# Token mixes with one product each, and expert weights that may come from DRAM, in a macaron transformer on one Trainium2 core

## The chip, the cores and the metric

The kernel runs on one core of one Trainium2 chip. The metric is the device time of one launch in microseconds (us). A core has five engines with instruction streams of their own: TensorE (PE, matrix products), VectorE (DVE), ScalarE (ACT), GpSimd (POOL) and SyncE (SP, which here only issues transfers). They wait for each other by semaphores. Data lie in DRAM, in the on-chip memory SBUF (128 partitions) and in PSUM (the 8 accumulator banks that PE writes). DMA transfers move data between DRAM and SBUF.

## The reference

The input has 8 sequences of 256 tokens with 128 features, so 2048 tokens. Six residual steps follow each other, each on a layer norm of the running `x`:

```
x = x + 0.5 * moe(layernorm(x))          # 8 experts, hidden 352, top 2 per token
x = x + attention(layernorm(x))          # 16 heads of 8, causal
x = x + 0.5 * moe(layernorm(x))          # same weights as the first
x = x + 0.5 * mix(layernorm(x))
x = x + shift(layernorm(x))              # 9 gated, rolled copies, then a layer norm
x = x + 0.5 * mix(layernorm(x))          # same weights as the first mix
```

The step that the change is mainly about is `mix`. Each token is blended with the token before it (zeros ahead of the first token of a sequence), feature by feature, with two different blends:

```
x_prev = concatenate([zeros, x[:, :-1]], axis=1)
xr = mu_r * x + (1 - mu_r) * x_prev
xk = mu_k * x + (1 - mu_k) * x_prev
r   = sigmoid(xr @ W_r.T)
k   = xk @ W_k.T
out = r * (square(relu(k)) @ W_v.T)
```

## The kernel before

**Tiling.** The tokens form four groups of 512 (`NG`), each held as `x[g]` with 4 tiles of 128 tokens (`GT`). Nearly every step works on one group. A product of 128 features by 512 tokens is one instruction of the program for PE, which the hardware runs as two, since the data are 32-bit floats.

**Order.** The program first describes all steps as operations with an engine, an expected duration, the operations they need and the buffers they take. `Work.issue` then lists them: it goes through the ready operations, takes the one that can start first by its own reckoning, and prefers higher ranks. The order on every engine is fixed by this. An `either` operation goes to ScalarE or VectorE, whichever would be done first (`LEAN` adds to the reckoned time of an engine). Numbers in `BIAS` shift the rank of whole groups: entries 0 to 3 rank the four groups in the last part of the program, 4 and 5 the two parts of the second expert layer's routing, 6 the later part of the first one's. Where PE would stand still by the reckoning, `keep_warm` inserts filler products (`pw`) into an unused bank. Line numbers in the profile are those of one helper (L71) for nearly all instructions, so tiles are known by their names.

**Expert layers** (`moe_route`, `moe_plan`, `moe_experts`, `moe_back`). Tokens are routed, a plan (counts, places, lookup products `pi`) sorts them by expert into 36 tiles of 128 rows, and each tile consists of two halves of 64 rows, called units, each with one expert. Rows are fetched by indirect DMA on POOL's queue (`xs`), transposed and scaled (`nT`), multiplied by the gate and up weights (`pg`, `pu`), gated (`sg`, `hid`), transposed (`ph`, `hT`), multiplied by the down weights (`po<-dw,hT` and `po<-wd,hT`) and stored to DRAM (`ys`, on SP's queue). Later `moe_back` fetches each token's two rows (`back`, POOL's queue) and adds them to `x`. The plan has two parts: the first two groups' tokens fill 12 tiles, which can start before the other groups are routed.

All weights of all experts stay in SBUF: `gu` (128 x 8 x 704) and `dw` (128 x 8 x 384). The first unit of a tile reads its expert's weights there, by a register on PE. For the second unit, `copied` (line 1073) copies the expert's weights into `wg` or `wd` (three buffers each) by an `either` operation, with the expert number in a register of the copying engine. There are 72 + 72 such copies, 89 on ScalarE and 55 on VectorE.

`dw`'s rows lie in three blocks of 128 that start at `HC` = (0, 128, 224), so the third block starts with rows 224 to 255, which are already in the second. Therefore `dw[0:32, :, 2, :]` is set to zero on VectorE and the third block is loaded for partitions 32 to 127 alone.

**Mix** (line 1569). For one group: moments, a power on POOL, normalising on ScalarE into `y`, transposing on PE into `pt`, and a copy into `yTs` (one zero column ahead of each sequence), so that the token before is the same data one column to the left. The blend lies in the weights: `mix_weights` (line 1802) makes `wkp`, `wkk`, `wrp` and `wr` once, with six VectorE steps, and each of the two results is a sum of two products:

```
for k, weight in enumerate((wkp, wkk)):
    nc.tensor.matmul(
        pk, lhsT=weight, rhs=yT.out[:, :, k : k + S], start=(k == 0), stop=(k == 1)
    )
```

`pr` is built in the same way, in 4 tiles with two products each. Then `rk` (relu) and `ka` (square) on ScalarE, `pv` on PE, `r` (tanh) on ScalarE, `rv` on VectorE, and an addition into `x[g]` on POOL. There are eight mixes: two for each group.

**Shift** (line 1653). Nine gate products `pgt`, each with a tanh on ScalarE and a product with the shifted values on VectorE (`p` or `q`). `FOLD[g]` says how they are summed: a number m means that m of them are first added pairwise on POOL, and each such sum then goes through `total` on PE, four products with the identity that add into the bank `po`. Group 0's (4, 4, 1) has three `total`s and six POOL additions.

Of the kernel before, what the change touches and what calls it, by code (L numbers as in the profile page):

```python
# [13 lines left out]
AF = mybir.ActivationFunctionType  # L14
# [20 lines left out]

BIAS = (32.0, 24.0, 8.0, 17.0, 27.0, 19.0, -1.0)
HC = (0, 128, 224)
ROUND = float(3 * 2**22)  # L40
NH = 16
# [9 lines left out]


ASIDE = ((3,), ())
FOLD = ((4, 4, 1), (2, 2, 2, 2, 1), (4, 4, 1), (2, 2, 2, 2, 1))


TB, DB = 1, 1
LEAN = {"act": 0.0, "dve": 0.15}


class InOrder:
# [47 lines left out]
class Op:  # L109
    def __init__(self, engine, us, do, needs, takes, uses, lag, spare):  # L110
        self.engine, self.us, self.do, self.lag, self.spare = engine, us, do, lag, spare
        self.takes, self.uses = takes, uses
        self.needs = [n for n in needs if n is not None]
        self.out, self.end, self.rank, self.back = None, None, None, 0.0
        self.strips = False
        self.choice = None


class Work:
# [14 lines left out]
    def op(self, engine, us, do=None, needs=(), takes=(), uses=(), lag=0.0, spare=0):  # L134
# [8 lines left out]
        self.ops.append(op)  # L143
        return op

    def either(self, act, dve, do, *needs, **kw):

        op = self.op("act", min(act, dve), None, needs, **kw)
        op.choice = {"act": act, "dve": dve}
        op.do = lambda: do(op.engine)  # L150
        return op
# [6 lines left out]
    def start(self, op):  # L158
        if op.choice is None:
            return self.start_on(op)  # L160
        best = None
        for engine, us in op.choice.items():
            op.engine = engine
            t = self.start_on(op)
            if t is None:
                return None
            us += LEAN.get(engine, 0.0)
            if best is None or t + us < best[0]:
                best = (t + us, t, engine)
        op.engine, op.us = best[2], op.choice[best[2]]  # L170
        return best[1]


# [98 lines left out]
def tile_macaron(ctx: ExitStack, tc: tile.TileContext, a: dict, out: bass.AP):  # L272
# [9 lines left out]
    def ctile(name, shape, dtype=F32):  # L282
        return const.tile(shape, dtype, tag=name, name=name)
# [10 lines left out]
        nc.sync.dma_start(out=x[g], in_=xv[g])  # L294
    gu = ctile("gu", [P, E, 2 * HID])
    dw = ctile("dw", [P, E, len(HC), P])

    nc.vector.memset(dw[0:32, :, 2, :], 0.0)
    half = E // 2
    nc.sync.dma_start(out=gu[:, 0:half, :], in_=a["guT"][:, 0:half, :])  # L300
    nc.sync.dma_start(out=dw[:, :, 0:2, :], in_=a["dwT"][:, :, 0:2, :])
    nc.sync.dma_start(out=dw[32:P, :, 2, :], in_=a["dwT"][32:P, :, 2, :])
    nc.sync.dma_start(out=gu[:, half:E, :], in_=a["guT"][:, half:E, :])


# [8 lines left out]
    rest = ctile("rest", [P, width])  # L314
    wd, wup, wuv, wo, wr, wkk, wv, vw, gw = (rest[:, c] for c in parts.values())
    wup = wup.rearrange("p (h r) -> p h r", r=32)
    wkp, wrp = ctile("wkp", [P, P]), ctile("wrp", [P, P])
    gamma = ctile("gamma", [P, P])
    beta = ctile("beta", [P, P])

# [16 lines left out]
    with nc.allow_low_precision("zeros and ones"):  # L337
# [34 lines left out]
    nc.vector.tensor_scalar(ha, ha, -0.5, 2.0, ALU.max, ALU.min)  # L372
    nc.vector.tensor_scalar(ha, ha, 0.5, None, ALU.mult)

    spare = ctile("spare", [P, 1])
    nc.scalar.activation(spare, one8[:, 0:1], AF.Silu)

# [10 lines left out]
        buffers={  # L388
            "b": 8, "xs": 3, "nT": 3, "y": 2, "nTr": 1, "sg": 2, "hid": 2, "hT": 2, "ys": 4,
            "at": 2, "ata": 1, "back": 2, "cT": 2, "av": 2, "o": 2, "oT": 2, "qk": 2, "ep": 4, "mtmp": 2,  # L390
            "t": 11, "q": 10, "p": 4, "mix": 2, "yTs": 2, "yTg": 2, "wg": 3, "wd": 3, "vT": 2,
        },
        free={"pool": 3.3, "dve": 3.3, "act": 2.5, "sp": 3.5, "pe": 2.6},
    )
# [14 lines left out]
    def copies(engine, dst, src):  # L409
        if engine == "act":  # L410
            nc.scalar.copy(dst, src)
        else:
            nc.vector.tensor_copy(dst, src)
# [6 lines left out]
    def wtile(tag, name, shape, dtype=F32):  # L420
        return wk.tile(list(shape), dtype, tag=tag, name=name, bufs=len_of[tag])
# [641 lines left out]
    def moe_tile(r, plan, k, nT, nb, j, pus, turned, downs, numbers):  # L1063
# [7 lines left out]


        def copied(engine, tag, src, width):
            e = {"act": nc.scalar, "dve": nc.vector}[engine].number(
                r["expert"][0:1, 2 * k + 1 : 2 * k + 2]
            )
            dst = wtile(tag, tag, (P, width))
            src = src[:, bass.ds(e, 1)].rearrange("p o h -> p (o h)")
            copies(engine, dst, src)
            return dst  # L1080

        gb, db = Buf("wg"), Buf("wd")
        gates = w.either(
            1.1, 0.9, lambda e: copied(e, "wg", gu, 2 * HID), plan["experts"], weights,
            *pus[-3:-2], takes=[gb],
        )
        backs = w.either(
            0.84, 0.74, lambda e: copied(e, "wd", dw.rearrange("p e c d -> p e (c d)"), len(HC) * P),
            plan["experts"], weights, *pus[-3:-2], takes=[db],
        )  # L1090

# [477 lines left out]
    def mix(g, n):  # L1569

        token = Buf("mix")
        y, filled = norm(
            g, n, "t", lambda: stile("t", "y"), switched, split=0, takes=[token]
        )
        b1, yb = Buf("b"), Buf("yTs")
        pt = w.pe(0.44, lambda: transposed(filled[0].out), *filled, takes=[b1], uses=[y], spare=1)

        def keep(engine):
            yT = stile("yTs", "yTs", (P, 2, S + 1))
            if engine == "act":  # L1580
                nc.scalar.activation(yT[:, :, 0:1], one8[:, 0:2].unsqueeze(2), AF.Copy, scale=0.0)
            else:
                nc.vector.memset(yT[:, :, 0:1], 0.0)
            copies(engine, yT[:, :, 1 : S + 1], pt.out.rearrange("p (b t) d -> p b (t d)", b=2))
            return yT

        yT = w.either(0.8, 0.76, keep, pt, takes=[yb], uses=[b1])
        b2, b3, b4 = Buf("b"), Buf("b"), Buf("b")


        def keys():
            pk = bank([P, 2, S], "pk")
            for k, weight in enumerate((wkp, wkk)):
                nc.tensor.matmul(
                    pk, lhsT=weight, rhs=yT.out[:, :, k : k + S], start=(k == 0), stop=(k == 1)
                )
            return pk.rearrange("p b s -> p (b s)")

        def receptances():
            out = bank([P, GT, P], "pr")  # L1600
            for t in range(GT):
                for k, weight in enumerate((wrp, wr)):
                    at = (t % 2) * P + k
                    nc.tensor.matmul(
                        out[:, t, :], lhsT=yT.out[:, t // 2, at : at + P], rhs=weight,
                        start=(k == 0), stop=(k == 1),
                    )
            return out

        def outcomes():  # L1610
            out = bank([P, GT, P], "pv")
            for t in range(GT):
                nc.tensor.matmul(
                    out[:, t, :], lhsT=ka.out[:, bass.ts(t, P)], rhs=wv, start=True, stop=True
                )
            return out

        pk = w.pe(1.76, keys, yT, weights_mixed, takes=[b2], uses=[yb], spare=2)
        pr = w.pe(1.8, receptances, yT, weights_mixed, takes=[b3], uses=[yb], spare=1)
        rkb, rrb, kab, rvb = (Buf("t") for _ in range(4))  # L1620

        def bent(name, src, function, shape):
            dst = stile("t", name, shape)
            nc.scalar.activation(dst, src, function, scale=0.5)
            return dst

        rk = w.act(
            0.6, lambda: bent("rk", pk.out, AF.Relu, (P, GT * P)), pk, takes=[rkb], uses=[b2]
        )
        r = w.act(  # L1630
            0.6, lambda: bent("r", pr.out, AF.Tanh, (P, GT, P)), pr, takes=[rrb], uses=[b3]
        )

        def square():
            ka = stile("t", "ka", (P, GT * P))
            nc.scalar.square(ka, rk.out)
            return ka

        ka = w.act(0.55, square, rk, takes=[kab], uses=[rkb])
        pv = w.pe(0.9, outcomes, ka, takes=[b4], uses=[kab])  # L1640

        def receptance():
            rv = stile("t", "rv")
            nc.vector.scalar_tensor_tensor(rv, r.out, 1.0, pv.out, ALU.add, ALU.mult)
            return rv

        rv = w.dve(0.7, receptance, r, pv, takes=[rvb], uses=[rrb, b4])
        changes(g, w.pool(
            1.3, lambda: nc.gpsimd.tensor_tensor(x[g], x[g], rv.out, ALU.add), rv,
            *tokens[g].given, *tokens[g].read, uses=[rvb, token],  # L1650
        ))
# [147 lines left out]

    rest_loaded = w.sp(1.5, load_rest, *(r0["stored"][g] for g in first), lag=8.0)  # L1800

    def mix_weights():

        for to, own, mu in ((wkp, wkk, mu_k), (wrp, wr, mu_r)):
            nc.vector.tensor_scalar(to, own, mu, None, ALU.mult)
            nc.vector.tensor_tensor(to, own, to, ALU.subtract)
            nc.vector.tensor_tensor(own, own, to, ALU.subtract)

    moe_plan(r0, False)
    w.back = -BIAS[6]  # L1810
    for g in range(len(first), NG):
        moe_route(g, r0)
    moe_plan(r0, True)
    w.back = 0.0
    weights_mixed = w.dve(2.0, mix_weights, rest_loaded, fewer, r0["plan"][1]["slots"])
    for groups in (first, list(range(len(first), NG))):
        moe_weights(groups, r0, r0["plan"][1]["taken"])
    stored = moe_experts(r0, [[1, 1, 2, *turns(r0["few"] - 4)], turns(TILES - r0["few"])])
# [97 lines left out]
```

## Time and profile before

| | us |
|---|---|
| median of 3 runs | 506.69 (506.56 to 506.85) |
| profiled execution | 506.38 |
| its span, first to last instruction | 504.6 |
| PE busy | 485.7 |
| VectorE busy | 355.0 |
| ScalarE busy | 285.0 |
| POOL busy | 225.3 |
| first expert product `pg` starts | 32.7 |
| first `pk` of a mix starts | 385.4 |
| last expert tile's products end | about 410 |
| last `total` ends | 485.2 |

The profile describes one execution. Durations of single instructions are read from it, and matmuls are pipelined, so the distance from start to start counts rather than the duration. Us from the span's start tell where a stretch lies. "Granted clock" is the share of full clock that TensorE was given.

### The profile page before, as it was taken

How to read it: one execution, taken by the hardware profiler on the slowest of the kernel's cores; microseconds unless marked ns; L12 is line 12 of the kernel's file. 1: busy time of each engine (PE TensorE's matmuls, PEld its weight loads, DVE VectorE, ACT ScalarE, POOL GpSimd, SP SyncE). 2: the span in 40 equal slices, each digit the busy share in tenths (PEclk: the TensorE clock that was granted, in tenths of full speed). 3: DMA queues.
4: the chain of work that ended last, by engine and by line, in shares of the span. 5: the costliest groups of instructions: out<-in, count | busy, mean ns of one | idle time of the engine just before them, and what ended most of it. 6: DMA issues, size and time to landing. Idle time of an engine off the chain costs nothing.

```text
span 504.6 us, 13830 instructions
## 1 busy us (share of the span) xinstructions
PE 485.7 (96%) x5199; PEld 317.9 (63%) x5199; DVE 355.0 (70%) x1207; ACT 285.0 (56%) x589; POOL 225.3 (45%) x240
## 2 busy tenths in 40 slices
PE   7979999999999999999999999799999999999995
PEld 4525667665676667776777766566665664665773
DVE  7847777678757886678786267946777657998561
ACT  3337666575365464455556567346767756557452
POOL 7154588472016500000037000278776858866362
PEclk9869999999999999999999799789999999999998
DMA  8841222221001100000202001032232211000001
GB/s 269 303 137 38 65 58 62 72 59 45 12 22 49 40 1 3 4 22 2 66 17 62 11 2 43 13 84 62 49 75 58 58 33 38 0 2 0 21 22 42
DMA packets 25984, 25.53 MB, mean 51 GB/s; under 512 B 3872, under 2 KB 23328, under 8 KB 25504
## 3 DMA queue, kind: packets, MB, share of 16 engines
q1 hardware_dynamic: 20368, 15.21, 9.8%
q0 software_dynamic: 4352, 8.92, 6.8%
q8 instruction: 42, 0.69, 0.5%
q10 hardware_dynamic: 1200, 0.53, 0.4%
q14 instruction: 22, 0.18, 0.1%
HBM read 16.78 MB, written 8.91 MB: 51 GB/s over the span
## 4 chain that ended last, share of the span: by engine, by line
PE 77%; DVE 13%; issue 3%; POOL 2%; DMA 2%; ACT 1%; POOLq 0%; DVEq 0%
PE sc L71 17%; PE po L71 16%; PE pg L71 9%; PE pu L71 9%; PE ph L71 5%; PE pt L71 5%; PE pgt L71 3%; PE pr L71 3%; PE pk L71 2%; DVE st L71 2%; PE pv L71 2%; DVE stats L71 2%; PE pj L71 2%; POOL back L71 2%; DMA xs<-rows,take 1%
## 5 line engine op out<-in xcount | busy, mean ns | idle before, releaser
L71 POOL DMA_INDIRECT xs<-rows,take x72 | 70.2, 975 | 48.7 <-issue 15.1
L71 POOL DMA_INDIRECT back<-ys,slot x64 | 61.9, 967 | 55.1 <-issue 45.2
L71 ACT ACTIVATE ep<-sc 128x512 f32<-128x512 f32 x96 | 52.3, 594 | 53.3 <-PE sc L71 53.3
L71 POOL TENSOR_TENSOR stats<-stats,minus_half 128x4 f32<-128x4 f32 x28 | 29.1, 1038 | 105.0 <-DVE stats L71 104.2
L71 PE MATMUL pg<-gu,nT 128*64 x144 | 58.3, 487 | 0.2
L71 PE MATMUL pg<-wg,nT 128*64 128x352 f32 x144 | 58.3, 487 | 0.0
L71 PEld LDWEIGHTS sc<-kT,qT 32*128 32x128 f32 x768 | 46.1, 186 | 19.1 <-issue 16.6
L71 PE MATMUL sc<-qT,kT 32*128 32x128 f32 x768 | 57.9, 288 | 0.1
L71 PE MATMUL pu<-gu,nT 128*64 x144 | 56.1, 472 | 0.3 <-PE pi L71 0.3
L71 PE MATMUL pu<-wg,nT 128*64 128x352 f32 x144 | 56.1, 472 | 0.0
L71 PE MATMUL sc<-kT,qT 32*128 32x128 f32 x768 | 55.5, 284 | 0.0
L71 PE MATMUL po<-dw,hT 128*64 x432 | 55.4, 279 | 0.0
L71 PE MATMUL po<-wd,hT 128*64 128x128 f32 x432 | 55.4, 279 | 0.0
L71 ACT ACTIVATE sg<-pg 128x352 f32<-128x352 f32 x72 | 33.3, 462 | 37.9 <-PE pg L71 25.9
L71 PEld LDWEIGHTS po<-dw,hT 128*64 128x64 f32 x432 | 48.6, 139 | 8.5 <-issue 6.4
L71 DVE TENSOR_REDUCE mtmp<-sc 128x4 f32<-128x512 f32 x64 | 41.4, 683 | 16.9 <-PE sc L71 16.8
L71 PEld LDWEIGHTS sc<-qT,kT 32*128 32x128 f32 x768 | 48.4, 190 | 3.4 <-issue 2.7
L71 PEld LDWEIGHTS po<-wd,hT 128*64 128x64 f32 x432 | 48.7, 139 | 0.0
L71 DVE TENSOR_TENSOR hid<-sg,pu 128x352 f32<-128x352 f32 x72 | 36.6, 515 | 15.9 <-PE pu L71 8.4
L71 ACT COPY wg<-gu 128x704 f32 x45 | 35.0, 779 | 13.8 <-PE pu L71 7.2
L71 PE MATMUL pgt<-yTg,rest 128*128 128x512 f32 x72 | 34.1, 600 | 1.1 <-DVE p L71 0.9
L71 PE MATMUL ph<-ident,hid 128*128 128x128 f32 x216 | 32.3, 285 | 0.3 <-DVE hid L71 0.3
(225 smaller groups left out, 1067.4 us busy)
## 6 DMA issues: line engine op xcount, KB each, us to landing
ys<-ys SPq DMA_DIRECT2D x72, 64.0 KB, 1.6
gu<-in_guT SPq DMA_DIRECT2D x2, 1408.0 KB, 8.4
rest<-in_rest SPq DMA_DIRECT2D x1, 1280.0 KB
xs<-rows,take POOLq DMA_INDIRECT x72, 2.5
x<-in_x SPq DMA_DIRECT2D x4, 256.0 KB
dw<-in_dwT SPq DMA_DIRECT2D x1, 1024.0 KB
rows<-rows SPq DMA_DIRECT2D x2, 512.0 KB
back<-ys,slot POOLq DMA_INDIRECT x64, 2.6
```

Source lines behind the costliest of these rows:

```text
L71: ins = do(*args, **kw)
```

## The change

Four things are changed.

1. **Mix.** `yTs`, `wkp`, `wrp` and `mix_weights` go. Two blended token tiles, `xk` and `xr`, are made in SBUF for each mix, in two steps each: `earlier_token` (on ScalarE or VectorE) writes the token before, times one minus mu, with zeros ahead of the first; `own_token` (VectorE) adds the token itself times mu, read from `pt`. `pk` is then one product, and `pr` one for each of the four tiles. One small step on VectorE (`less`) makes 1 - mu at the start.
2. **Weights of second units.** `copied` gets a third possibility, SP: a transfer from DRAM straight into `wg` or `wd`, with the expert number in a register of SP. The ordering reckons 1.9 and 1.2 us on SP for them, 2.6 us more until they land, and `LEAN` subtracts 2.5.
3. **`dw`.** Its DRAM image has the zeros for the overlapping rows, so the `memset` goes, and `dw` is loaded whole by one transfer.
4. **Numbers.** `BIAS` and `FOLD` are new, and `yTs` has four buffers in place of two.

In the order that results, 20 of the 144 weight copies are on SP (4 `wg`, 16 `wd`), 75 on ScalarE and 49 on VectorE. `earlier_token` is 11 times on ScalarE and 5 times on VectorE. There are 21 `total`s in place of 16, and 15 POOL additions in place of 20. Fillers `pw` are 100 in place of 94; behind the last `total` there are 29 in place of 18.

```diff
-BIAS = (32.0, 24.0, 8.0, 17.0, 27.0, 19.0, -1.0)
+BIAS = (25.0, 33.0, 10.0, 5.0, 15.0, 53.0, -5.0)
...
-FOLD = ((4, 4, 1), (2, 2, 2, 2, 1), (4, 4, 1), (2, 2, 2, 2, 1))
+FOLD = ((2, 2, 2, 1, 1, 1), (2, 2, 2, 1, 1, 1), (4, 4, 1), (2, 2, 2, 1, 1, 1))
...
-LEAN = {"act": 0.0, "dve": 0.15}
+GATES, BACKS, LANDING = 1.9, 1.2, 2.6
+LEAN = {"sp": -2.5, "act": 0.0, "dve": 0.15}
...
-    nc.vector.memset(dw[0:32, :, 2, :], 0.0)
...
-    nc.sync.dma_start(out=dw[:, :, 0:2, :], in_=a["dwT"][:, :, 0:2, :])
-    nc.sync.dma_start(out=dw[32:P, :, 2, :], in_=a["dwT"][32:P, :, 2, :])
+    nc.sync.dma_start(out=dw, in_=a["dwT"])
...
+            if engine == "sp":
+                src = {"wg": a["guT"], "wd": a["dwT"].rearrange("p e c d -> p e (c d)")}[tag]
             src = src[:, bass.ds(e, 1)].rearrange("p o h -> p (o h)")
-            copies(engine, dst, src)
+            if engine == "sp":
+                nc.sync.dma_start(out=dst, in_=src)
+            else:
+                copies(engine, dst, src)
...
-        yT = w.either(0.8, 0.76, keep, pt, takes=[yb], uses=[b1])
+        def by_own(name, own, other):
+            cb = Buf("yTs")
+            def earlier_token(engine):
+                c = stile("yTs", name, (P, 2, S))
+                src = pt.out.rearrange("p (b t) d -> p b (t d)", b=2)[:, :, 0 : S - 1]
+                if engine == "act":
+                    nc.scalar.activation(
+                        c[:, :, 0:1], one8[:, 0:2].unsqueeze(2), AF.Copy, scale=0.0
+                    )
+                    nc.scalar.activation(c[:, :, 1:S], src, AF.Copy, scale=other)
+                else:
+                    nc.vector.memset(c[:, :, 0:1], 0.0)
+                    nc.vector.tensor_scalar(c[:, :, 1:S], src, other, None, ALU.mult)
+                return c
+            c = w.either(0.8, 0.76, earlier_token, pt, takes=[cb], uses=[b1])
+            def own_token():
+                nc.vector.scalar_tensor_tensor(
+                    c.out, pt.out.rearrange("p (b t) d -> p b (t d)", b=2), own, c.out,
+                    ALU.mult, ALU.add,
+                )
+                return c.out.rearrange("p b s -> p (b s)")
+            return w.dve(0.7, own_token, c, uses=[b1, cb]), cb
+        xk, xkb = by_own("xk", mu_k, less_k)
+        xr, xrb = by_own("xr", mu_r, less_r)
...
+            nc.tensor.matmul(pk, lhsT=wkk, rhs=xk.out, start=True, stop=True)
...
+                nc.tensor.matmul(
+                    out[:, t, :], lhsT=xr.out[:, bass.ts(t, P)], rhs=wr, start=True, stop=True
+                )
```

## The prediction

> **What bounds the kernel now.** I read the page's head first, then its busy line, then one table by stretches, then the chain that ended last near the end.
>
> ```profile
> span 504.6 us, 13830 instructions
> PE 485.7 (96%) x5199; PEld 317.9 (63%) x5199; DVE 355.0 (70%) x1207; ACT 285.0 (56%) x589; POOL 225.3 (45%) x240
> PEclk9869999999999999999999799789999999999998
> ```
>
> TensorE (PE) is busy for 96% of the span, so time is mostly PE time. The clock row has dips, and the share is an average, so each stretch is looked at alone. In the table, the numbers behind a stretch are its length, then busy us of PE, weight loads, VectorE (DVE), ScalarE (ACT) and GpSimd (POOL), then granted clock, DMA share and GB/s.
>
> ```profile
> 24.00:31.00 7.00, 4.82 (x18) 1.68 (x16) 3.75 (x20) 1.72 (x3) 3.19 (x4) 0.74 0.85 260
> 282.50:290.00 7.50, 7.50 (x71) 5.15 (x72) 0.69 (x1) 3.26 (x7) 0.00 (x0) 0.55 0.01 2
> 320.00:331.00 11.00, 10.06 (x66) 6.92 (x65) 7.61 (x42) 3.79 (x8) 3.36 (x4) 0.54 0.08 21
> 384.00:410.00 26.00, 25.97 (x227) 18.00 (x226) 17.68 (x57) 16.96 (x42) 15.29 (x16) 1.00 0.20 54
> 410.00:425.00 15.00, 14.30 (x54) 7.48 (x50) 8.45 (x33) 10.67 (x24) 12.24 (x13) 1.00 0.16 45
> 425.00:460.00 35.00, 33.54 (x159) 20.93 (x159) 32.90 (x107) 20.96 (x49) 25.43 (x23) 1.00 0.00 1
> 460.00:485.00 25.00, 25.00 (x145) 18.23 (x144) 15.93 (x44) 12.91 (x25) 15.45 (x14) 1.00 0.04 11
> 485.00:504.60 19.60, 13.89 (x84) 9.56 (x82) 6.28 (x29) 7.48 (x17) 5.00 (x5) 0.93 0.13 40
> ```
>
> The reader is to see four things. 384 to 410 (end of the second expert layer, with the first two mixes between its tiles) and 460 to 485 are gapless on PE at full clock: PE work cut there is time. In 425 to 460 VectorE is busy 32.9 of 35, nearly as tight as PE. From 485 on a chain through several engines sets the end. And twice PE runs at about half clock, behind the end of attention and in the second expert plan.
>
> ```profile
> 478.01 0.89 PE po L71 x8
> 478.91 1.72 PE pk L71 x4
> 480.62 1.78 PE pr L71 x16
> 482.41 0.89 PE pv L71 x8
> ```
>
> This piece of the chain prices the products: `po` x8 is one `total` (four products with the identity, two instructions each) at 0.89; `pk` with two weights 1.72; `pr` with two weights 1.78. One product each is therefore 0.86 and 0.89.
>
> **The sum.** It is made against the profiled execution, 506.38 us (span 504.6, 1.78 around it); the median 506.69 lies 0.31 above, which I add at the end.
>
> *Products.* A mix loses 0.86 + 0.89 = 1.75 us of PE. There are eight. The instruction order keeps two ahead of the last expert tile (gapless stretch): -3.5. Four lie between there and the last `total`: -7.0. But FOLD raises the `total`s from 16 to 21 (64 to 84 products), all in that stretch: 5 x 0.89 = +4.45; and the fillers `pw` there go from 3 to 5 at 0.216, +0.4. Net there -2.1, not -7. The last two mixes lie behind the last `total`, in the closing chain, where PE waits with 18 fillers (29 after). There a mix now needs one more VectorE step (0.68 plus hand-over, about +0.75) ahead of `pk`, and has `pv` earlier: `pk` start to `pv` start was 3.6 (1.72 + 1.78 and a little), and becomes `pk` 0.86, `rk` 0.60 and `ka` 0.63 with hand-overs about 0.55, 2.65. Together -0.2. Sum of PE terms: -3.5 - 2.1 - 0.2 = -5.8. Its cover is that VectorE and ScalarE feed PE as densely as before.
>
> *VectorE.* Added: 16 `own_token` steps and 16 `earlier_token` steps in place of 8 copies. Nearest row for `own_token`, also PSUM and SBUF in, 128x512:
>
> ```profile
> L71 DVE SCALAR_TENSOR_TENSOR p<-pgt,vT 128x512 f32<-128x512 f32 x32 | 20.5, 681 | 6.8 <-ACT pgt L71 4.1 <-POOL q L71 2.6
> ```
>
> 0.68 each, about 0.62 from start to start (four of them in a row took 2.47). So 16 x 0.62 = 9.9 us in all; 5.0 for the four mixes between the expert tiles and the last `total`. `earlier_token` is an `yTs` copy (0.58 on ScalarE, 0.69 on VectorE): ScalarE gets 11 (from 7), VectorE 5 (from 1), 3 of them in the tail (from 1), +1.4 there. So VectorE gets 6.4 us more in a stretch of 75 where it has 57.3, of which some 6.5 are stalls beside POOL (four `x<-back` steps took 3.16 instead of 1.13; steps on 4 elements 1.2 instead of 0.17). The stalls shrink, because POOL loses 5 of 20 additions of 1.27. VectorE at 61 to 64 of 73 is still under PE (68), but two of the mixes fall where it was 94% busy. Charge between 0 (all in the slack of 460 to 485) and 6.4 (nothing hides); I take +1.5, two mixes' 2.5 less about 1 of stalls, as its row there has 2.1 us free.
>
> *Weights.* 20 of 144 copies move to SP (4 `wg`, 16 `wd`); ScalarE drops 14 and VectorE 6. They cost 0.78 / 0.59 (`wg`) and 0.51 / 0.38 (`wd`), but PE was gapless in those stages, so the relief is worth nothing by itself. On SP each fetch brings a register load, a wait for a freed buffer, and a DMA; behind it queue the `ys` stores, which nobody needs before `moe_back` gathers them. No row shows a fetch of 352 or 192 KB; the nearest, 64 KB, took 1.6 (`ys`) to 2.5 (`xs`), and 1408 KB of `gu` 8.4. So I estimate 2 to 4 us from these, and a buffer is freed about two tiles (5 us) ahead of its use: 0, bounds 0 and +3 (most fetches a bit late).
>
> *Start.* The first fetches (second tile, 352 + 192 KB) are issued as soon as the expert numbers are known, now earlier, about 24. There the DMA engines are 0.85 busy, and the first gathered rows land at 31.4, when that ends. 0.54 MB at 260 GB/s is 2.1 us. PE waits for the gather, 2.2 us in this trace. If the gather stands behind the fetch, +2.1; if they share fairly, near 0 (below nothing is possible, as the first copies no longer wait till 28.6, but they did not gate). I take +1.0. The dropped `memset` of `dw` (0.9) and `mix_weights` (six steps, 1.8, at 54) lie beside a full PE: 0. The `dw` load has 0.13 MB more, while the queue ran dry at 20: 0.
>
> *Order.* The new BIAS puts the first part of the second plan some score batches later, and leaves more expert tiles to cover its second part, where PE stalled. Lost today: 0.45 x 7.5 = 3.4 and 0.46 x 11 = 5.1 to the half clock, 0.9 idle. Bounds -5 and +4; I take -1, since the order has two more tiles' products behind the lookups (`pi`) before the next gather is needed, yet attention's end now runs with fewer tiles beside it.
>
> The Trainium skill, page "TensorE: Matmul & The Clock Gate", Part 1, says that the array falls to half clock after an idle window of about 3.4 us and needs a busy one to come back. That speaks against thinning PE's work: one such window in the tail, an estimate from that page, would add 1.7 us (504.1 in place of 502.4). This trace agrees in kind (0.55 and 0.54 above) but shows 1.00 in all of 384 to 485, so the sum has nothing for it.
>
> Sum: -5.8 + 1.5 + 0 + 1.0 - 1.0 = -4.3; 506.38 - 4.3 = 502.1, and with the 0.31 **502.4**.
>
> **Rivals.** *A: VectorE becomes the bound, slower.* Place: the stretch that was 425 to 460. All 6.4 us come on top and PE's -2.1 there is lost: -3.5 - 0.2 + 6.4 + 1.0 - 1.0 = +2.7, 509.4. It decides once the charge exceeds about 5.8. For: 32.9 of 35. Against: 9 us free in 460 to 485, fewer stalls, and eleven first halves go to ScalarE, 60% busy there.
> *B: the new order costs.* The later first plan leaves PE with neither scores nor tiles behind attention; one more stretch like 282 to 290 (3.4) in place of the -1: 502.4 + 4.4 = 506.8, no change. For: VectorE stood still in that stretch, so the chain was already latency. Against: the first gathers are still ahead of attention's last products.
> *C: the new order pays.* Both half-clock stretches mostly go, 5 instead of 1, and the start costs 0: 502.4 - 5 = 497.4. For: they follow from waits that extra tiles would fill.
> *D: the fetches do not take work away.* With 20 of 144 moved that is nearly so, and is priced in.
>
> **Chances.** Forecast 0.60, A 0.15, B 0.10, C 0.15. The forecast's own range is 499 to 506 (start 0 to 2.1, VectorE 0 to 4, order -2 to +1). To hold 8 in 10 the range goes to 496 (C with VectorE hidden) and to 508.5 (into A). Faster by over 0.2% (1 us, about what a measurement of this kernel can tell from no change): C, nearly all of the forecast, a third of B: 0.77. Within: 0.05. Slower: A, some of B and the forecast's edge: 0.18.
>
> **What would show it.** Right: `pk` 0.86 and `pr` 0.89 per mix in the chain, PE's busy time down by about 8 (14.0 less 4.45 and six more fillers); in the last 80 us VectorE under 95% with PE gapless at clock 1.00; first `pg` about a microsecond later. Wrong: PE waiting for VectorE `xk` or `xr` or for a DMA into `wd` or `wg` for several us in total; a first `pg` unchanged or 2 us later; a half-clock stretch in the tail; the two half-clock stretches gone (C) or longer (B).

## The result, and the profile after

The changed kernel takes 499.0 us (median of 4 runs, 497.8 to 501.1); before takes 506.7. The ratio on record is 0.9861 (95% interval 0.983 to 0.9892), so 7.0 us less where 4.3 were forecast; the two medians lie 7.7 apart. A second sample (E12 below) gave 498.9 against 506.3, ratio 0.9861 (0.9823 to 0.9899). The medians here and below leave out runs that stand apart: one of before at 510.8, and those over 1.5% above the fastest of their kernel (in E12 one at 503.7).

The head of the page after, in the order of the page shown for before:

```profile
span 496.1 us, 13845 instructions
...
PE 469.7 (95%) x5165; PEld 310.1 (63%) x5165; DVE 363.8 (73%) x1227; ACT 277.2 (56%) x575; POOL 218.6 (44%) x235
...
PEclk9889999999999999999999999599999999999998
```

PE's busy time fell by 16.0, twice the 8 that the forecast named as a sign of being right. Busy time contains the half-clock stretches, so this is not work alone. The table by stretches, cut at the places that answer to those of before:

```profile
24.00:31.00 7.00, 3.99 (x18) 1.38 (x15) 5.06 (x29) 2.14 (x4) 3.73 (x4) 0.89 0.89 293
276.90:284.40 7.50, 7.50 (x156) 5.87 (x154) 1.62 (x8) 5.55 (x11) 2.96 (x4) 1.00 0.08 20
313.00:324.00 11.00, 10.09 (x73) 7.59 (x75) 8.45 (x45) 3.01 (x7) 3.19 (x4) 0.57 0.05 14
403.10:418.10 15.00, 13.75 (x43) 6.60 (x42) 10.62 (x32) 11.17 (x28) 12.23 (x13) 1.00 0.15 44
418.10:453.10 35.00, 33.94 (x196) 24.34 (x196) 33.47 (x117) 23.56 (x53) 20.77 (x18) 1.00 0.01 1
453.10:474.90 21.80, 21.80 (x120) 15.24 (x119) 16.40 (x45) 10.98 (x23) 14.60 (x13) 1.00 0.09 25
474.90:496.10 21.20, 13.45 (x73) 7.99 (x71) 10.58 (x38) 8.27 (x18) 4.65 (x5) 0.93 0.09 26
```

The reader sees that the half-clock stretch at the end of attention is gone (1.00 where before had 0.55), that the one in the second plan is still there (0.57), and that VectorE is as tight in the middle of the tail as it was (33.5 of 35); whether it is the bound there is what E8 asks. POOL is 4.7 less busy there than in the 35 us of before.

It helps to cut both spans into four stages: the *start* up to the first `pg`; the *lead* from there to the end of the last expert tile; the *tail* to the end of the last `total`; and the *close*.

| us | start | lead | tail | close |
|---|---|---|---|---|
| before | 32.7 | 377.5 | 75.0 | 19.4 |
| after | 32.1 | 371.0 | 71.8 | 21.2 |
| after, repeated (E12) | 33.1 | 370.4 | 71.7 | 21.2 |
| forecast of the change | +1.0 | -4.5 | -0.6 | -0.2 |

The forecast's -4.5 is two mixes and the order, its -0.6 the four mixes, the five `total`s, the fillers and the charge for VectorE. Each stage has its own error: the lead and the tail gave more, the close gave back 1.8. The lead of before, then of the changed kernel:

```profile
32.70:410.20 377.50, 372.33 (x4639) 248.38 (x4638) 267.05 (x834) 221.15 (x453) 152.27 (x152) 0.97 0.15 40
32.10:403.10 371.00, 362.23 (x4613) 243.31 (x4613) 268.69 (x834) 211.26 (x430) 152.01 (x152) 0.98 0.19 52
```

Counting half of each half-clock stretch as lost, an estimate from the clock records, the lead lost 10.9 to half clock in before and 6.8 in the changed kernel. So up to 4.1 of its 6.5 may lie in the clock.

### The profile page after: what moved, and what is told of

Read it like the earlier page. It is cut to its first block, busy times and chain, and to the rows that moved or that the text cites. A ratio compares the mean times of both kernels' runs of the same rounds, so it can differ in the third digit from the quotient of the medians.

```text
span 496.1 us, 13845 instructions
## 1 busy us (share of the span) xinstructions
PE 469.7 (95%) x5165; PEld 310.1 (63%) x5165; DVE 363.8 (73%) x1227; ACT 277.2 (56%) x575; POOL 218.6 (44%) x235
## 4 chain that ended last, share of the span: by engine, by line
PE 73%; DVE 12%; POOL 6%; issue 3%; ACT 2%; DMA 2%; POOLq 0%; ACTq 0%; DVEq 0%
PE sc L72 17%; PE po L72 16%; PE pg L72 8%; PE pu L72 7%; PE pt L72 5%; PE ph L72 5%; PE pgt L72 4%; POOL back L72 2%; PE pv L72 2%; PE pr L72 2%; PE pj L72 2%; DVE at L72 2%; PE pw L72 2%; DMA xs<-rows,take 1%; PE pl L72 1%
## 5 line engine op out<-in xcount | busy, mean ns | idle before, releaser
L72 POOL TENSOR_TENSOR stats<-stats,minus_half 128x4 f32<-128x4 f32 x28 | 29.0, 1037 | 88.1 <-DVE stats L72 84.9
L72 PE MATMUL pg<-gu,nT 128*64 x144 | 56.8, 477 | 0.5 <-ACT nT L72 0.5
L72 PE MATMUL pg<-wg,nT 128*64 128x352 f32 x144 | 56.8, 477 | 0.0
L72 PE MATMUL sc<-qT,kT 32*128 32x128 f32 x768 | 56.4, 283 | 0.2
L72 PEld LDWEIGHTS sc<-qT,kT 32*128 32x128 f32 x768 | 47.0, 186 | 3.3 <-issue 2.4
L72 ACT COPY wg<-gu 128x704 f32 x40 | 31.0, 778 | 10.9 <-PE pu L72 4.6
L72 PE MATMUL ph<-ident,hid 128*128 128x128 f32 x216 | 32.1, 286 | 0.1
```

Of the source, the lines that this page charges most:

```text
L72: ins = do(*args, **kw)
```

## The experiments

Theory 1 was that TensorE's work sets the pace and the parts of the change act separately. The rivals were that VectorE and POOL hide the products in the tail, that the fetches carry the gain, and, read from the trace after, that the new order carries it by taking away a half-clock stretch. Each part is first left out with the order free to change (E1 to E4, E9); then the order is held and one cost is moved (E6 to E8, E10, E11).

A "kernel with the order held" issues the same instructions in the same places on each engine but for the ones named, since the ordering still reckons with the durations of the changed kernel.

**E1, without the new mix** (the mix of before; the rest new)

```diff
-        pk = w.pe(0.88, keys, xk, rest_loaded, takes=[b2], uses=[xkb], spare=2)
+        pk = w.pe(1.76, keys, yT, weights_mixed, takes=[b2], uses=[yb], spare=2)
```

> The changed kernel with the mix of before (eight mixes with two products each, weights blended once); fetches, BIAS and FOLD stay new. The order up to the first mix is the same as in the changed kernel. Theory 1, TensorE sets the pace: two mixes more ahead of the last expert tile cost 2 x 1.75 = 3.5, four more behind it up to 7.0, and the closing chain gets 1.8 shorter: 499.0 + 3.5 + 7.0 - 1.8 = 507.7. Theory 2, VectorE was the bound in the densest stretch of the tail, so that a good part of the four mixes' gain was lost there: only the first 3.5 come back in full, 499.0 + 3.5 + (2 to 4) - 1.8 = 502.7 to 504.7.

Measured: 508.1, ratio 1.0019 (0.9993 to 1.0044). Its tail:

```profile
407.20:482.10 74.90, 74.66 (x389) 50.66 (x390) 52.11 (x173) 42.71 (x93) 45.50 (x41) 1.00 0.06 17
```

PE is busy 74.7 of 74.9: with two products per mix and 21 `total`s, the tail is pure PE time. The time agrees with theory 1, but the tail doesn't: it is only 3.1 longer than after, not 7.0. Of the rest, 3.0 is a longer lead, as forecast for two mixes, and some is a lower granted clock (0.962 to 0.975 in its runs, 0.973 to 0.980 in those of after). The profile is of a run at 505.7, below the median.

**E2, BIAS and FOLD alone**, and **E9, BIAS alone** (the kernel before with these numbers)

```diff
-BIAS = (32.0, 24.0, 8.0, 17.0, 27.0, 19.0, -1.0)
+BIAS = (25.0, 33.0, 10.0, 5.0, 15.0, 53.0, -5.0)
```

> The kernel before with the new BIAS and FOLD and nothing else. Theory 1, the order alone took away the half-clock stretch at the end of attention and the stalls of the second expert plan: the last expert tile ends about 3.4 earlier than in before, scores end 5 to 6 earlier, and the five more totals cost up to 4.45 in the tail: 506.7 - 3.4 + 4.45 = 507.7, and less where VectorE waits on POOL go with the five POOL additions. Theory 2, the fetches did it, by taking 20 copies off ScalarE and VectorE: the half-clock stretch at 282 to 290 stays, 506.7 + 4.45 = 511.2.

> The kernel before with the new BIAS alone (FOLD, mix and weight copies stay old). Theory 1, the new ranks are what moved the end of attention and the second plan: scores end about 5 to 8 earlier (at 279 to 282 in place of 287.2), the second plan's lookups end at 317 to 320 in place of 326.1, and the last expert tile about 6 earlier; the tail from there on stays near 75, since neither its products nor its totals change: 506.7 - 6 = 501, or less gain where the tail's order is worse. Theory 2, the order is worth nothing by itself and the gain lies in mix and FOLD: 506.7, scores end at 287.

Measured: E2 510.5, ratio 1.0075 (1.0052 to 1.0099); E9 509.4, ratio 1.0094 (1.0057 to 1.0131). Both are slower than before, which neither theory of E9 had. E9 at the end of attention, in its lead and in its tail, then E2 in its lead and in its tail:

```profile
276.00:291.00 15.00, 14.92 (x285) 12.14 (x274) 5.52 (x25) 10.46 (x21) 6.42 (x7) 1.00 0.11 28
...
33.00:411.10 378.10, 370.56 (x4643) 248.49 (x4643) 271.33 (x854) 216.94 (x450) 154.83 (x154) 0.98 0.16 40
411.10:489.50 78.40, 75.51 (x361) 47.94 (x362) 50.86 (x163) 42.23 (x90) 49.57 (x43) 0.98 0.06 17
```
```profile
32.10:401.90 369.80, 362.99 (x4636) 245.49 (x4636) 270.13 (x841) 215.27 (x446) 153.61 (x152) 0.99 0.15 41
401.90:482.80 80.90, 77.32 (x394) 51.80 (x395) 56.25 (x186) 44.26 (x96) 46.60 (x42) 0.98 0.05 15
```

In E9 the scores end at 283.8 in place of 287.2 and the clock there is 1.00, as the theory of the order says. Yet the lead is 378.1, no shorter than before. Work has only moved: some routing products that ran ahead of the last score now run behind it, and the products of two expert tiles that ran ahead of the last lookup now run behind that. The last lookup ends 3.1 earlier (323.0), and the stretch from there to the last expert tile grows from 84.1 to 88.1. The earlier milestones were not a gain. And the tail grows to 78.4, the close to 21.3.

E2 gives another picture of the lead. With the old mix and without fetches it is 369.8, 7.7 shorter than in before and no longer than in the changed kernel; the scores end at 279.3, and the half-clock stretch at 282 to 290 is gone, as theory 1 had it, though the time is near theory 2's. Its tail of 80.9 and its close of 21.7 take the gain back. The two profiles are not quite comparable: E2's is of its fastest run (506.2, median 510.5), E9's of the slowest that counts (512.5, median 509.4), and by the same estimate as above E2's lead lost 5.1 to half clock and E9's 9.4. So the theory that the new numbers by themselves make a faster kernel is refuted by the times. That their order shortens the lead is not refuted, and E2 speaks for it; how much stays open.

**E3, without fetches** (all 144 copies on ScalarE and VectorE, order free) and **E6, the same with the order held**

```diff
-        op.choice["sp"] = sp
-        op.lags = {"sp": LANDING}
```

> The changed kernel with all 144 weight copies on ScalarE and VectorE again; mix, BIAS and FOLD stay new. Theory 1, the fetches are worth nothing (the sum of the prediction): 499.0, within 1. Theory 2, they brought a part of what exceeded the prediction, by taking 20 copies off two engines around the second plan and at the start: 501 to 503, with the first pg not earlier than in before and the granted clock of 15 to 45 back at 0.77.

For E6 the 20 operations stay where SP had them, and are issued to ScalarE or VectorE:

```diff
+        def near(e):
+            return e if e != "sp" else "act" if w.free["act"] <= w.free["dve"] else "dve"
...
-            1.1, 0.9, GATES, lambda e: copied(e, "wg", gu, 2 * HID), plan["experts"], weights,
+            1.1, 0.9, GATES, lambda e: copied(near(e), "wg", gu, 2 * HID), plan["experts"], weights,
```

> The changed kernel with every instruction in the same place, but the 20 fetched weights copied from SBUF by ScalarE or VectorE (ten each) at the place where the fetch stood. Theory 1, the relief is worth nothing and the loss of the kernel without fetches came from another order: the time of the changed kernel within 1. Theory 2, the relief is worth something: ten copies on either engine, 10 x 0.55 each, that then stand in the way of sg, hid and hT: 2 to 5 more, with TensorE waiting for hT or nT in the expert layers. Start: the first fetch (352 KB) is gone there; if it delayed the first gathered rows, the first pg comes up to 2 earlier.

Measured: E3 509.8, ratio 1.0083 (1.005 to 1.0115). E5 to E8 ran on a chip on which before took 592.1; there the changed kernel had a ratio of 0.9885 (E5, below) and E6 had 0.9861 (0.9818 to 0.9903). With the order held, the runs overlap (581.3 to 587.2, and 580.0 to 587.1 in E5): copying the weights costs nothing that shows. The two intervals bound that only to about 4, and on a chip whose lead is 82 longer (below), where a small cost could hide; E6 was not run on an ordinary chip. On one, E3's profile speaks for it: no wait of PE over 0.2 is for a copy into `wg` or `wd`. The first `pg` came at 33.0 in both E5 and E6, so the fetches in front of the first gathers cost nothing either. E3's ratio is 0.022 above that of the changed kernel, about 11 us and so more than those 4: its loss is for the most part another order. Its tail is 77.0, 5.2 longer than that of the changed kernel. The waits of VectorE in E3 from 405.2 to 430, then those of PE in its tail, then PE's table:

```profile
DVE stats L72 <- POOL stats L72: 3.0, 1, 3.0
```
```profile
PE pw L72 <- DVE p L72: 4.6, 1, 4.6
```
```profile
415.00:423.00 8.00, 3.93 (x10) 1.52 (x9) 4.10 (x7) 2.90 (x8) 6.93 (x7) 1.00 0.14 42
423.00:426.50 3.50, 2.95 (x8) 1.00 (x8) 3.50 (x5) 2.19 (x6) 2.32 (x2) 0.51 0.00 0
```

The power `stats` of one group's norm stands on POOL behind eight gathers `back` of another (409.6 to 418.4, about 1.25 apart). VectorE's next step on `stats` waits 3.0 for it, and all of VectorE's queue with it; the `p` steps come late, PE stands still for 4.6, and then gets half clock for 3.4. E2 has the same 3.0 in the same place. In the changed kernel both powers are issued (at 404.5 and 405.8) ahead of the gathers (from 407.0), and VectorE waits 1.1. So far as this wait goes, this is what the fetches are worth here: by other reckoned times they led to an order in which POOL's queue holds up VectorE less. The other 2 or 3 of E3's loss, in the lead, are not followed up.

**E4, without the new FOLD**, and **E11, with more `total`s** (order of E11 unchanged until well into the tail)

```diff
-FOLD = ((2, 2, 2, 1, 1, 1), (2, 2, 2, 1, 1, 1), (4, 4, 1), (2, 2, 2, 1, 1, 1))
+FOLD = ((4, 4, 1), (2, 2, 2, 2, 1), (4, 4, 1), (2, 2, 2, 2, 1))                      # E4
+FOLD = ((2, 2, 1, 1, 1, 1, 1), (2, 2, 1, 1, 1, 1, 1), (4, 4, 1), (2, 2, 2, 1, 1, 1)) # E11
```

> The changed kernel with the FOLD of before: 16 totals and 20 POOL additions in place of 21 and 15. Theory 1, TensorE sets the pace in the tail: five totals less are 4.45 less of it, 499.0 - 4.45 = 494.6. Theory 2, with one product per mix TensorE waits in the tail for sums that POOL and VectorE make, and VectorE stalls beside POOL: the totals were free, 499 to 502, with TensorE idle in the stretch from the last expert tile to the last total.

> The changed kernel with FOLD (2, 2, 1, 1, 1, 1, 1) for groups 0 and 1: two more totals on TensorE, two additions fewer on POOL. The order is the same until into the second group's gates. Theory 1, a total costs the tail its 0.89: the stretch from the last expert tile to the last total grows from 71.7 to 73.5. Theory 2, a total costs less than the POOL addition that it replaces (1.27, with VectorE stalled beside it), while TensorE still waits there: the stretch shrinks to between 70 and 71.7.

Measured: E4 505.9, ratio 0.9974 (0.9951 to 0.9997); E11 499.8, ratio 0.9905 (0.9869 to 0.9941). The tail of E4 and its fillers (from PE's groups there), then the fillers of the changed kernel's tail, then the tail of E11:

```profile
407.20:482.60 75.40, 70.75 (x334) 43.47 (x335) 60.98 (x179) 45.39 (x102) 50.69 (x44) 1.00 0.06 18
```
```profile
L72 PE MATMUL pw<-before,ones_b 128*128 128x512 bf16 x26 | 6.6, 379 | 0.0
```
```profile
L72 PE MATMUL pw<-before,ones_b 128*128 128x512 bf16 x6 | 1.8, 379 | 0.0
```
```profile
405.40:477.10 71.70, 70.72 (x370) 47.52 (x369) 61.44 (x195) 44.81 (x99) 45.01 (x40) 1.00 0.06 17
```

With 16 `total`s PE has 4.45 less to do, and yet the tail is 3.6 longer: PE fills 26 slots with `pw` and is idle for another 4.7. With 21 it has 6 fillers and 2.3 idle. With 23 the tail is the same again (71.7); PE's idle time there falls to 1.0 and its work rises by as much. The rest of E4's loss lies in its start and lead (33.7 and 373.5); the order also changed near the end of the lead. So a `total` is not a cost of 0.89 here: it takes the place of an addition of 1.27 on POOL, and pays until PE's waiting is used up, which happens at 21 to 23. It does not pay in every order: with the old mix the same FOLD goes with a longer tail (80.9 in E2, 78.4 in E9). By which wait an addition delays the tail is only argued: PE's longest waits in E4's tail are for VectorE's `p` (2.2) and `xr` (1.2), and VectorE stands beside a POOL that is busy 50.7 there, 47.6 in the changed kernel.

**E5, the changed kernel on the chip of E6 to E8; E7, a second product in each `pk` and `pr`; E8, half of the blend** (order held)

```diff
+                for k, weight in enumerate((wr, none)):                                # E7, pk alike
...
+                if name == "xr":                                                       # E8
+                    return xk.out
```

> The changed kernel itself, beside the next three on one chip. All theories: 497.8 to 501.1 as before. What is asked is the spread, and whether it follows the number of half-clock stretches (each 3.4 long, so at most 1.7 lost in each).

> The changed kernel in the same order, with a second product with a zero matrix in each pk and pr, so TensorE's work is that of before and VectorE's and ScalarE's that of after. Theory 1, TensorE sets the pace in the tail: 2 x 1.75 ahead of the last expert tile's end, 4 x 1.75 behind it, and up to 1.7 in the closing chain: +10.5 to +12. Theory 2, TensorE waited in the tail anyway for what VectorE makes, so products are partly hidden: +3.5, then 2 to 5, then 0.9: +6.4 to +9.4.

> The changed kernel in the same order, without the two steps that make xr: pr reads xk, so half of the blend is left out. VectorE loses 8 x 0.74 for own_token and the earlier_token steps it has (0.75 each), ScalarE the rest. Theory 1, the blend lies beside TensorE's work but for what the sum charged (1.5 for both halves): 0.5 to 1 less in the tail. Theory 2, VectorE sets the pace between the last expert tile and the last total: the tail shortens by 2 to 4. In the closing chain both say about 1.4 less (xr stands ahead of pk there), if pk waits for it.

Measured: E5 585.9 (ratio 0.9885, 0.9827 to 0.9943), E7 595.0 (1.0065, 1.0034 to 1.0096), E8 579.4 (0.9839, 0.978 to 0.9898). The chip is slower in the lead alone; tail and close of E5 take the same 71.7 and 21.2 as elsewhere, so these two stages can be compared across chips. Tail and close of E7, then of E8:

```profile
493.90:570.40 76.50, 75.25 (x394) 51.16 (x395) 60.20 (x192) 45.83 (x102) 47.46 (x42) 1.00 0.06 16
570.40:594.30 23.90, 16.43 (x94) 10.58 (x91) 10.49 (x38) 8.51 (x18) 4.67 (x5) 0.98 0.08 23
```
```profile
484.80:555.80 71.00, 69.41 (x355) 46.18 (x356) 58.47 (x187) 43.90 (x96) 47.63 (x42) 1.00 0.06 18
555.80:576.20 20.40, 13.41 (x73) 8.09 (x71) 8.48 (x34) 7.39 (x16) 4.60 (x5) 0.93 0.09 26
```

The second products bring back 4.8 in the tail (not 7.0, and within theory 2's 2 to 5): PE is busy 5.9 more than in E5 and idle 1.1 less. In the close they bring back 2.7, more than either theory had. Half of the blend is worth 0.7 in the tail and 0.8 in the close (1.4 said), so both halves come to about 1.4 in the tail, an estimate by doubling. That is theory 1's size: VectorE does not set the pace there.

**E10, fillers ahead of the second plan's lookups** (order held)

```diff
+                for _ in range(11 if whole and r is r1 else 0):
+                    nc.tensor.matmul(
+                        room, lhsT=ones_b, rhs=before.unsqueeze(1).to_broadcast([P, GT, P]),
+                        start=True, stop=True,
+                    )
```

> The changed kernel in the same order, with eleven filler products (0.216 each) put into the bank of pi ahead of the first lookup of the second plan of the second expert layer, where TensorE stands idle for 2.44. Theory 1, that idle window is what brings the half clock of 10.2 behind it: it goes or shrinks, 1.7 to 4.5 less than the changed kernel (0.983 to 0.978 of before where that has 0.986 to 0.989). Theory 2, the half clock there comes from the thin lookups themselves, and stays: no change, or up to 0.5 more where the fillers delay the first lookup.

Measured: 500.1, ratio 0.993 (0.989 to 0.997). From the last score to the last lookup, first in the changed kernel, then in E10:

```profile
281.60:319.30 37.70, 32.67 (x335) 22.46 (x337) 31.29 (x150) 21.45 (x40) 14.28 (x15) 0.91 0.28 78
```
```profile
283.30:321.00 37.70, 35.00 (x348) 23.07 (x348) 31.10 (x150) 21.25 (x40) 14.36 (x16) 0.96 0.29 78
```

The half-clock stretch shrank from 10.2 to 6.8, as theory 1 said (it is 10.2 or more in every other profile), but the stage takes 37.7 in both, which is theory 2's time. The fillers stand where PE waited for VectorE's `at` (3.0 in the changed kernel, 0.6 here), and the lookups come no earlier. What causes the half clock that is left stays open.

**E12, the changed kernel repeated**

> The changed kernel itself once more, for a larger sample beside before on one chip. In the runs so far the time falls by 1.1 to 1.4 for each 0.0034 of mean granted clock (one stretch of 3.4 at half clock), and at a clock of 0.970 before is at 505.5 to 506.7. Theory 1, about half of the first measured 7.7 was a better clock in the first runs of the changed kernel (0.973 to 0.980 against 0.967): at equal clock it is 4 to 5.5 ahead, and where before is near 506, its median is 500 to 502. Theory 2, the change itself keeps the clock up (one half-clock stretch less behind attention in every run): its clock stays above that of before by 0.006 or more and the median at 498 to 499.7.

Measured: 498.9 (ratio above), granted clock 0.973 to 0.980. Together with the first four runs there are nine of the changed kernel, beside 64 of before on ordinary chips. Sorted by the mean granted clock of the run, the average times are:

| granted clock | before | after |
|---|---|---|
| 0.966 to 0.968 | 506.6 (28 runs) | none |
| 0.969 to 0.971 | 506.6 (14) | none |
| 0.972 to 0.974 | 505.6 (10) | 499.7 (5) |
| 0.975 to 0.977 | 504.7 (7) | 499.4 (2) |
| 0.978 and above | 500.6 (5) | 497.0 (2) |

At equal clock the change is worth 3.6 to 5.9, from few runs of the changed kernel. The remaining 1.1 to 3.4 of the 7.0 would then lie in the clock, which averaged 0.971 in before and 0.976 in after. Both theories hold in part. That the change itself raises the clock is not shown: E10 and E11, whose leads have the same order, had runs from 0.966 to 0.982, and E11 averaged 0.9725 where before averaged 0.9729 beside it (their times 500.3 and 504.6 on average).

## Why the prediction was right, and where its steps were not

**Products.** The work was counted rightly, and the lead's two mixes came as forecast (3.0 between E1 and after, 3.5 said). The four mixes of the tail were mis-sized: "Four lie between there and the last `total`: -7.0" became 4.8 by E7. The condition that the prediction itself put there, "that VectorE and ScalarE feed PE as densely as before", does not hold in full: without the second products PE waits, as its 2.3 idle and 6 fillers show. Of the 7.0, PE's busy time accounts for 5.9, and 1.1 of that was waiting which the second products had filled.

**FOLD.** This term is the largest error: "+4.45" and 0.4 for fillers, charged to PE, against a tail that is 3.6 shorter with the new FOLD (E4 to after, order free) and unchanged by two more `total`s (E11). The prediction did see that POOL loses five additions, but credited it with only 1 us of stalls.

**VectorE.** The charge of +1.5 agrees with the estimate from E8 (about 1.4), though `own_token` takes longer than the row that priced it:

```profile
L72 DVE SCALAR_TENSOR_TENSOR xr<-pt,few,xr 128x512 f32<-128x512 f32 x8 | 6.0, 744 | 0.0
L72 DVE SCALAR_TENSOR_TENSOR xk<-pt,few,xk 128x512 f32<-128x512 f32 x8 | 5.9, 743 | 0.8 <-ACT xr L72 0.7
```

0.74 in place of 0.68. Rival A did not come: PE stayed the bound. But the mix then gives the tail only 4.8 - 1.4 = 3.4 (3.1 between E1 and after), which is what BIAS alone takes from it (E9): with the old FOLD (E4) the tail is 75.4, as long as in before.

**Weights.** 0 agrees with E6, to within its 4 and on the slower chip. The prediction did not see that 20 operations with other reckoned times change the order of everything behind them, which is where E3 lost.

**Start.** +1.0 was too much. The first `pg` was 0.6 earlier in one profile, 0.4 later in the other, and E5 and E6 do not differ.

**Order.** -1.0 stands against some 3 in the lead (6.5 less the mixes' 3.0 to 3.5), which come with the whole set of changes and hold the better clock of these runs. What the new numbers alone do to the lead stays open: 0.6 longer in E9's profile, 7.7 shorter in E2's. What BIAS does in the tail was missed: +3.4 (75.0 to 78.4 in E9). The sum 78.4 - 3.4 (mix) - 3.6 (FOLD) = 71.4 comes near the measured 71.8, but that these parts add is not shown: from E9 by E2 and E1 to the changed kernel the tail goes 78.4, 80.9, 74.9, 71.8, so on that way FOLD costs 2.5 and the change from E2 to E1, which brings the fetches, gives 6.0. Rival C gave the closest time (497.4), but its cause came only by half: of the two half-clock stretches the one at the end of attention went, and the one in the second plan is 10.2 long in both. B's stretch of 3.4 behind attention is in E1 (from 296.7) and E9 (from 301.0), but not in the changed kernel.

**Close.** -0.2 was right for the mix (21.6 in E1, 21.2 after), and the +1.8 comes with BIAS (21.3 in E9): the last two groups' mixes now stand closer together (their `pk` 4.0 apart, before 7.1). The chain of the changed kernel there, with start, length and what ran:

```profile
479.63 0.45 PE pt L72 x4
...
480.10 0.70 ACT xk L72
...
480.82 0.75 DVE xr L72
481.57 0.66 DVE xk L72
482.23 0.08 DVE stats L72
...
482.37 1.10 PE pk L72 x2
483.47 0.89 PE pr L72 x8
484.36 0.45 PE pt L72 x4
```

`pk` x2 and `pr` x8 with 0.89 each are the single products as priced (`pk`'s 1.10 holds its start-up). But the last group's `stats` step stands behind two blend steps on VectorE, and its transpose `pt` behind the other group's `pk` and `pr`.

**The half clock.** The Trainium skill, page "TensorE: Matmul & The Clock Gate", Part 1, says half clock follows an idle window of about 3.4 us, and that the window runs freely, so the same kernel varies from run to run. The tail of the changed kernel kept 1.00, so nothing was due in the sum. In E3 half clock does follow idle time (4.6 idle, then 3.4 at 0.51), and so it does in the tails of E2 and E9, there behind 3.3 and 2.8 of idle. But the prediction's reading that before "agrees in kind" does not hold. Its half clock at the end of attention came with PE busy 7.50 of 7.50 and no wait of PE of over 0.2 from 268 to 295, and in its second plan PE's longest wait was 1.6. Idle time does not explain the first, and no idle of 3.4 stands ahead of the second; the measurement decides.

**The total.** That the time fell inside the range is in part luck. FOLD was charged 4.9 that it did not cost in this order, and the lead gave 2.0 more than its terms; against that the tail's mixes gave 2.2 less, and BIAS cost the tail 3.4 and the close 1.8 for which the sum had no term. What held is the mechanism named first: products cut where PE has no gaps save time, as E1 and E7 show.

## What to carry to other kernels

Cost a step that moves work between engines by both queues: an operation that "only adds" work to the busiest engine can pay where it takes an operation off a queue that the others wait for, until the idle time is used up. Where a planner decides the order, leave one part out twice, once with the order free and once with it held (E3 and E6); the difference between the two is the order's share, and here it was larger than the part's own cost. An earlier milestone in a trace is a gain only if the work ahead of it did not just move behind it.

## What had not been expected of the hardware

- The half-clock stretches in all these profiles last 3.4, 6.8, 10.2 or 13.7, but for the one that the end of the span cuts. The times of runs of one kernel follow them: before ran between 499.6 and 506.7 on one chip with mean clocks of 0.986 to 0.966. A line through the 64 runs of before gives 1.0 less for each 0.0034 of clock, which is one stretch of 3.4 (1.3 in the nine runs of after).
- On one chip the lead took 452.9 in place of 371.0 with the same program (E5), while tail and close took the same. The granted clock in it was 0.91 in place of 0.98, and PE's longest waits there were `PE po` for nothing that the profile shows (16.8 in 17 waits). What differs on that chip stays open.
- A VectorE step can take far longer beside a POOL addition, but not every step does. In E4 three `x<-d` steps overlapped one and took 0.34, 0.34 and 1.35 us; the other thirteen took 0.34 to 0.35, and so did all sixteen of the changed kernel, none of which overlapped an addition. There the six `x<-back` steps that did took 0.34 to 2.72, the other 58 at most 0.40. The `p` steps, one of whose inputs lies in PSUM, took 0.67 to 0.69 beside additions and away from them.
